# Layer 1's bias sums placed amid the first block's products, and its second factor transposed into other PSUM pools

## The chip, the cores and the metric

The kernel runs on one core of one Trainium2 chip. The metric is the device time of one execution in microseconds (us); the figure used is the median of several executions. The core's engines are named as the profile names them: PE (TensorE, with PEld for its weight loads), DVE (VectorE), ACT (ScalarE), POOL (GpSimd) and SP (SyncE, which here only issues transfers). Each engine works through its own queue of instructions; semaphores order them against one another.

## The reference

A stack of four graph layers over 128 graphs of 64 nodes with 512 features, all in float32. Every layer starts with a layer norm and a ReLU and adds its result to x. The two layers that the change touches:

```python
# layer 0: h = relu(layernorm(x))
qk = h @ Wqk;  q, k = split(qk);  v = h @ Wv
agg = einsum('bij,bjd->bid', adj, k * mask)
w = mask * einsum('bid,bid->bi', q, agg) / sqrt(512)
x = x + softmax(w, axis=1)[:, :, None] * v

# layer 1: h = relu(layernorm(x))
query = h @ Wq.T + bq;  key = h @ Wk.T + bk;  value = h @ Wv.T + bv
weight = adj * exp(query @ key.T)
x = x + (weight / weight.sum(axis=2, keepdims=True)) @ value
```

Layer 2 is an attention with eight heads, layer 3 a three-step graph propagation. Neither is touched.

## The kernel before, in words

The 8192 tokens are cut into 32 blocks of 256 tokens (two tiles of 128). Blocks go through layers 0 and 1 in pairs, in the order of the list `steps`: layer 0 of blocks 0 and 1, layer 1 of blocks 0 and 1, layer 0 of blocks 2 and 3, and so on. Layers 2 and 3 follow. A block's products with 512x512 weights are made by seven half-size products with sums (a scheme of Strassen's kind): `sums` (L204) forms the sums of the activations on POOL, `formed` (L86) those of the weights, and `Product` (L223) issues the matmuls, with its two PSUM tiles called ab and dc. Of a product, `first` and `second` are the early matmuls, after which `keep_ab` (L276) saves a part through ACT (p, L280) and DVE (u, L281); `late` (L296) adds the rest and `store` (L300) writes the result through ACT (L302), DVE (L303 to L305) and POOL (L306). The late matmuls of a tile can't start before `keep_ab` has read it. `side_by_side` (L346) issues two such products together; its list `between` holds actions for three places amid them: after the first product's early part, ahead of the first late part, ahead of the second.

A query and its key meet only in a product, so both projections of a layer are folded into one weight. That is setup work. For layer 0 it stands in `setup0` (L438), for layer 1 in `setup1` (L446). `setup1` is a generator. Its first part loads the two 512x512 factors qT and kT, the two bias rows (b1qk) and the value weight. The factors go into the weight slots 4 and 5, which layer 0's factors used, so their loads wait until layer 0's fold has been made. Its second part

- makes nine sums on DVE (L467), each a product of 128x512 elements with an accumulated sum: four columns of qT with the key's bias (u1), four of kT with the query's bias (c1), and the product of the two biases (d1);
- sends c1 through DRAM and back as a row on all partitions (L473, L475);
- transposes both factors on PE (`transpose_weight`, L411: 16 transposes into four PSUM tiles, tw_q and then tw_k, which four copies put back into the factor in place, two on DVE, L422, and two on ACT, L420);
- multiplies them (`folded`, L424: four PSUM tiles pf of 512 columns, each from four matmuls, copied out half by ACT, L434, and half by DVE, L435);
- forms the weight sums on POOL and asks for layer 2's weights.

The nine sums share a buffer tag ("agg") with the neighbour sums of layer 0. PSUM is cut into three pools: `ps_tr` with two tiles (tag "tr": transposed activations, layer 0's neighbour sums pa), `ps_mm` with four (tag "mm": ab and dc of the products, tw and pf of the setup), and `ps_sc` with two (tag "sc": scores, sums over a graph).

In the main loop the second part of `setup1` is asked for after layer 0 of block 0 and ahead of layer 0 of block 1:

```python
for i, (layer, b) in enumerate(steps):
    if i == 1:
        made1 = next(setup)
```

Layer 0's own end of a block (`layer0_end`, L526: a sum over the graph on PE, sm_w, L400, then the softmax on ACT and DVE and the addition to x) is kept in the list `open_end` and issued amid the next block's products, so for block 0 amid block 1's. Within what the program text allows, a scheduler places the instructions in each engine's queue. In the queues before, PE has for this stretch: the late products of block 0, tw_q, pa of block 1, sm_w of block 0, tw_k, pf, and the products of block 1. DVE has: the last sums of block 0's products, L511, the nine sums with wd (L518) behind the first of them, the copies of q, the start of the softmax, the copies of k. ACT has: two copies of q, the copies of pa, the softmax with two copies of k amid it.

Of the kernel before, what the change touches and what calls it, by code (L numbers as in the profile page):

```python
# [8 lines left out]
FP = mybir.dt.float32  # L9
AF = mybir.ActivationFunctionType  # L10
ALU = mybir.AluOpType
AX = mybir.AxisListType

P = 128
N = 64
D = 512
K = D // P
# [8 lines left out]
def kernel(ctx: ExitStack, tc: tile.TileContext, a: dict, out: bass.AP):  # L26
# [7 lines left out]
    nc = tc.nc  # L34
# [7 lines left out]
    med = ctx.enter_context(tc.tile_pool(name="med", bufs=3))  # L42
    snap = ctx.enter_context(tc.tile_pool(name="snap", bufs=2))
    small = ctx.enter_context(tc.tile_pool(name="small", bufs=3))
    ps_tr = ctx.enter_context(tc.tile_pool(name="ps_tr", bufs=2, space=bass.MemoryType.PSUM))
    ps_mm = ctx.enter_context(tc.tile_pool(name="ps_mm", bufs=4, space=bass.MemoryType.PSUM))
    ps_sc = ctx.enter_context(tc.tile_pool(name="ps_sc", bufs=2, space=bass.MemoryType.PSUM))
# [32 lines left out]
    def slot(place: int, name: str):  # L80
        return wpool.tile([P, 7, 2, F], FP, tag=f"w{place}", name=name)
# [3 lines left out]
    def formed(w, engine):  # L85
        for to, x, y in sums_of_weights:  # L86
            engine.tensor_tensor(w[:, to], w[:, x], w[:, y], ALU.subtract)
# [3 lines left out]
    def later(w):  # L91

        chores.extend((w, s) for s in sums_of_weights)
# [7 lines left out]
    def fetched(name: str, place: int, queue):  # L101
        w = slot(place, name)
        for i in range(2):
            for j in range(2):
                queue.dma_start(
                    w[:, quarters[i][j]],
                    a[name][i * F : (i + 1) * F, j * F : (j + 1) * F].rearrange(
                        "(k p) o -> p k o", p=P
                    ),
                )  # L110
        return w
# [16 lines left out]
    def factor(ap, which: str, layer: int, queue):  # L128

        w = slot({"q": 4, "k": 5}[which], f"{which}_{layer}")  # L130
        w = w.rearrange("p s k o -> p (s k o)")[:, : K * D].rearrange("p (k o) -> p k o", k=K)
        for k in range(K):
            queue.dma_start(w[:, k, :], ap[k * P : (k + 1) * P, :])
        return w
# [4 lines left out]
    f0 = [  # L139
        factor(a["L0_Wqk"][:, i * D : (i + 1) * D], c, 0, queue)  # L140
        for i, (c, queue) in enumerate((("q", nc.scalar), ("k", nc.sync)))
    ]
# [254 lines left out]
    def graph_sums(e, cols: int, name: str):  # L397

        ps = ps_sc.tile([P, cols], FP, tag="sc", name=f"sm_{name}")
        nc.tensor.matmul(ps, ones_bd, e, start=True, stop=True)  # L400
        return ps
# [6 lines left out]
        return r  # L408


    def transpose_weight(w, name: str):  # L411

        pts = [ps_mm.tile([P, K, P], FP, tag="mm", name=f"tw_{name}_{m}") for m in range(K)]
        for k in range(K):
            for m, pt in enumerate(pts):
                nc.tensor.transpose(pt[:, k, :], w[:, k, m * P : (m + 1) * P], ident)
        for m, pt in enumerate(pts):
            flat = pt.rearrange("p k i -> p (k i)")
            if m % 2:
                nc.scalar.copy(w[:, m, :], flat)  # L420
            else:
                nc.vector.tensor_copy(w[:, m, :], flat)  # L422

    def folded(aT, bT, layer: int, place: int):  # L424

        m = slot(place, f"fold{layer}")
        for i in range(K):
            pm = ps_mm.tile([P, D], FP, tag="mm", name=f"pf_{layer}_{i}")
            for k in range(K):
                nc.tensor.matmul(  # L430
                    pm, aT[:, k, i * P : (i + 1) * P], bT[:, k, :],
                    start=(k == 0), stop=(k == K - 1),
                )
            nc.scalar.copy(m[:, quarters[i // 2][0], i % 2, :], pm[:, :F])  # L434
            nc.vector.tensor_copy(m[:, quarters[i // 2][1], i % 2, :], pm[:, F:])  # L435
        return m

    def setup0():  # L438
# [7 lines left out]
    def setup1():  # L446


        qT, kT = (factor(a[f"L1_W{c}"], c, 1, nc.sync) for c in "qk")

        bias = big.tile([P, 2, P, K], FP, tag="v", name="b1qk")
        for i, n in enumerate(("L1_bq", "L1_bk")):
            nc.sync.dma_start(
                bias[:, i], a[n].rearrange("(o p) k -> o p k", o=1).to_broadcast([P, P, K])
            )
        w1v = fetched("L1_Wv", 3, nc.sync)
        yield
        u = const.tile([P, K], FP, tag="u1", name="u1")
        cc = small.tile([P, K], FP, tag="cc", name="c1", bufs=1)
        d = const.tile([P, 1], FP, tag="d1", name="d1")  # L460
        for to, x, by in (
            *((u[:, k : k + 1], qT[:, k, :], 1) for k in range(K)),
            *((cc[:, k : k + 1], kT[:, k, :], 0) for k in range(K)),
            (d, None, 1),
        ):
            junk = med.tile([P, P, K], FP, tag="agg", name="bias1", bufs=2)
            nc.vector.scalar_tensor_tensor(  # L467
                junk, bias[:, 0] if x is None else x.rearrange("q (k p) -> q p k", k=K), 1.0,
                bias[:, by], ALU.mult, ALU.mult, accum_out=to,
            )  # L470

        crow = tc.dram_tile([1, D], FP, name="c1_row")
        nc.sync.dma_start(crow.rearrange("o (k p) -> p (o k)", p=P), cc)  # L473
        c1 = const.tile([P, 2, D + 1], FP, tag="u3", name="c1")[:, 0, :D]
        nc.sync.dma_start(c1, crow.to_broadcast([P, D]))  # L475
        for w, c in zip((qT, kT), "qk"):
            transpose_weight(w, f"{c}1")
        m = folded(kT, qT, 1, 2)
        formed(m, nc.gpsimd)
        formed(w1v, nc.gpsimd)  # L480
        w2 = [fetched(f"L2_W{c}", 4 + i, nc.sync) for i, c in enumerate("qk")]
        for w in w2:
            later(w)
        yield m, u, c1, d, w1v, w2
# [41 lines left out]
    def layer0_end(b: int, x, gv, w, wd):  # L526
        wrow = graph_sums(wd.rearrange("p t i -> p (t i)"), TT * N, f"w_{b}")
        mn = small.tile([P, TT], FP, tag="mx0", name=f"mn0_{b}")
        nc.vector.tensor_reduce(
            mn, wrow.rearrange("p (t i) -> p t i", t=TT), AX.X, ALU.min  # L530
        )
        nc.vector.tensor_tensor(w, w, mn, ALU.subtract)
        tot = small.tile([P, TT], FP, tag="tot", name=f"tot_{b}")
        for t in range(TT):
            nc.scalar.activation(
                wd[:, t, :], wrow[:, t * N : (t + 1) * N], AF.Exp, bias=mn[:, t : t + 1],
                scale=-1.0, accum_out=tot[:, t : t + 1],
            )
        ex = small.tile([P, TT], FP, tag="ex", name=f"ex_{b}")
        nc.scalar.activation(ex, w, AF.Exp, scale=-1.0)  # L540
        att = small.tile([P, TT], FP, tag="att", name=f"att_{b}")
        nc.vector.reciprocal(att, tot)
        nc.vector.tensor_tensor(att, att, ex, ALU.mult)
        for t in range(TT):
            nc.vector.scalar_tensor_tensor(
                x[:, t, :], gv[:, 1, t, :], att[:, t : t + 1], x[:, t, :], ALU.mult, ALU.add
            )
# [364 lines left out]

    prepare(0)
    transpose_weight(f0[0], "q0")
    turned(0)
    transpose_weight(f0[1], "k0")
    m0, msc = setup0()
    formed(w0v, nc.gpsimd)
    loaded[1] = load_x(1, x_d[rows(1), :], 0), load_adjT(1, 0)
    setup = setup1()  # L920
    next(setup)
    open_end = []
    for i, (layer, b) in enumerate(steps):
        if i == 1:
            made1 = next(setup)
        between = [[], [chore], []]
        for n, end in open_end:
            between[n].append(end)
        if i + 1 < len(steps):
            between[0].append(lambda: prepare(i + 1))  # L930
            between[2].append(lambda: turned(i + 1))
        else:
            between[0].append(lambda: prepare2(0))
            between[2].append(lambda: turned2(0))
        if layer == 0:
            softmax = layer0(b, *loaded[b], *normed[i], between)
            open_end = [(0, lambda b=b, softmax=softmax: layer0_end(b, *softmax))]
        else:
            attention = layer1(b, *loaded[b], *normed[i], between)
            open_end = [  # L940
                (1, lambda b=b, a=attention: layer1_end(b, loaded[b][0], *a, x1[b]))
            ]
        if i == len(steps) - 3:
            made2 = setup2()
# [7 lines left out]
    def layer3_step(b: int, ahead: bool = True):  # L952
# [20 lines left out]
    qk, ops = layer2_in(0, normed2[0], [  # L973
        [lambda: prepare2(1), chore], [*(end for _, end in open_end), chore], [lambda: turned2(1)]
    ])
# [8 lines left out]
    for b in range(n_blk):  # L984
        x = loaded2[b][0]
# [7 lines left out]
        if b + 1 < n_blk:  # L993
            qk, ops = layer2_in(b + 1, normed2[b + 1], [[], [lambda: chore(1 if b else 2)]])
# [99 lines left out]
```

## Time and profile before

| what | us |
|---|---|
| median of three executions | 2693.18 (2690.39 to 2693.68) |
| the profiled execution | 2690.4 |
| its span, from the first to the last instruction | 2688.6 |
| PE busy in the span | 2646.6 |
| layer 1's setup on PE, from tw_q to the first product of block 1 | 43.77 to 73.78 |

A line of the timeline gives the start, the duration, the engine, the line of the program and the operation, what is written and what is read, the shape and the count, and in brackets the idle time of that engine just before with what ended it. A line of the windows view gives a stretch, its length, the busy time of PE, PEld, DVE, ACT and POOL with the number of instructions, then PE's granted clock as a share of full speed, the share of time that the transfer engines were busy, and their rate in GB/s. A line of the waits view gives who waited, for whom, the time in all, how often, and the longest. A float32 matmul shows as two matmul records for each instruction of the program, a transpose as one. The end of a matmul record is modelled, so records that follow one another overlap a little.

### The profile page before, as it was taken

The page shows a single profiled execution, that of the slowest core. Times are in us where ns is not written, and L with a number is a line of the kernel's source. Part 1 is how long each engine was busy: PE and PEld are TensorE (multiplying, and loading weights), DVE is VectorE, ACT ScalarE, POOL GpSimd, SP SyncE. Part 2 cuts the span into 40 slices and gives each one's busy share as a digit, 9 for nine tenths or more (in the row PEclk, how much of TensorE's full clock was granted, in tenths as well). Part 3 has the DMA queues.
Part 4 walks back from the last instruction along what each step waited for, and adds up shares of the span by engine and source line. Part 5 has one row for each costly group of instructions (what it writes and reads, how often), then busy time and mean ns, then how long its engine had stood idle before and what let it go on. Part 6 is the DMA issues. An engine that isn't in the chain of part 4 may idle for free.

```text
span 2688.6 us, 52721 instructions
## 1 busy us (share of the span) xinstructions
PE 2646.6 (98%) x20752; PEld 2256.7 (84%) x20752; DVE 1682.3 (63%) x4398; ACT 942.7 (35%) x2290; POOL 1274.9 (47%) x1585
## 2 busy tenths in 40 slices
PE   8999999999999999999999999999999999999999
PEld 5888888888888888898999999999877777777776
DVE  5566666666666666555655655555666666666664
ACT  2333334333433333333333333333323333333332
POOL 3443333333334344655654565555564544444454
PEclk9999999999999999999999999999999999999999
DMA  4200111111101112111111111111211111111110
GB/s 155 69 35 34 34 34 35 42 43 37 47 34 34 34 66 78 37 52 37 39 45 44 39 37 52 37 39 52 72 50 46 56 51 51 51 51 51 51 50 32
DMA packets 103165, 129.81 MB, mean 48 GB/s; under 512 B 40834, under 2 KB 50050, under 8 KB 102916
## 3 DMA queue, kind: packets, MB, share of 16 engines
q1 hardware_dynamic: 102340, 125.38, 14.0%
q8 instruction: 163, 2.67, 0.4%
q10 hardware_dynamic: 576, 1.05, 0.1%
q14 instruction: 86, 0.70, 0.1%
HBM read 76.07 MB, written 50.34 MB: 47 GB/s over the span
## 4 chain that ended last, share of the span: by engine, by line
PE 77%; DVE 11%; DMA 5%; POOL 3%; ACT 2%; issue 2%; POOLq 0%; SPq 0%; ACTq 0%; DVEq 0%
PE ab_v L251 10%; PE ab_y L251 10%; PE dc_v L251 8%; PE dc_y L251 7%; PE ab_g L244 4%; PE ab_g L251 4%; DMA x<-x 4%; PE dc_g L244 3%; PE ab_q L244 3%; PE dc_g L251 3%; PE ab_k L244 3%; PE po L392 3%; PE tr L190 3%; PE dc_k L244 2%; PE dc_q L244 2%; DVE e L662 2%
## 5 line engine op out<-in xcount | busy, mean ns | idle before, releaser
L179 ACT ACTIVATE h<-x,nmr,rstd 128x512 f32<-128x512 f32 x256 | 194.4, 806 | 212.7 <-DVE nmr L174 208.8
L167 DVE BATCH_NORM_STATS2 stats<-x 128x6 f32<-128x512 f32 x256 | 167.3, 675 | 75.4 <-DMA x<-x 71.1
L172 POOL TENSOR_TENSOR rstd<-ve,neghalf 128x2 f32<-128x2 f32 x128 | 89.5, 699 | 260.8 <-DVE ve L170 260.5
L251 PE MATMUL ab_y<-L_Wk,hT 128*128 128x256 f32 x768 | 206.2, 391 | 3.6 <-DVE u_y L303 2.6
L251 PE MATMUL ab_v<-L_Wv,hT 128*128 128x256 f32 x768 | 202.8, 387 | 4.8 <-DVE stats L167 3.7
L251 PEld LDWEIGHTS ab_y<-L_Wk,hT 128*128 128x128 f32 x768 | 136.1, 190 | 75.9 <-issue 25.1
L251 PE MATMUL ab_v<-L_Wv,S 128*128 128x256 f32 x768 | 198.0, 381 | 0.0
L251 PE MATMUL ab_y<-L_Wk,S 128*128 128x256 f32 x768 | 197.9, 380 | 0.0
L251 PE MATMUL dc_v<-L_Wv,S 128*128 128x256 f32 x768 | 197.3, 380 | 0.0
L251 PE MATMUL dc_y<-L_Wk,S 128*128 128x256 f32 x768 | 193.8, 381 | 0.2 <-DVE u_y L851 0.2
L251 PEld LDWEIGHTS dc_y<-L_Wk,S 128*128 128x128 f32 x768 | 146.2, 191 | 21.4 <-DVE u_y L851 1.7
L251 PEld LDWEIGHTS ab_v<-L_Wv,S 128*128 128x128 f32 x768 | 146.8, 191 | 19.9
L872 POOL TENSOR_TENSOR tz<-tz,y 128x512 f32<-128x512 f32 x63 | 91.3, 1449 | 146.1 <-ACT tz L869 146.1
L251 PEld LDWEIGHTS dc_v<-L_Wv,S 128*128 128x128 f32 x768 | 143.8, 191 | 18.8 <-issue 0.8
L251 PEld LDWEIGHTS ab_y<-L_Wk,S 128*128 128x128 f32 x768 | 144.1, 191 | 18.1
L251 PEld LDWEIGHTS ab_v<-L_Wv,hT 128*128 128x128 f32 x768 | 136.5, 191 | 22.9 <-ACT qk L323 7.5
L190 PE MATMUL tr<-ident,h 128*128 128x128 f32 x1024 | 134.3, 275 | 0.4 <-ACT h L179 0.4
L190 PEld LDWEIGHTS tr<-ident,h 128*128 128x128 f32 x1024 | 119.4, 142 | 11.2 <-ACT h L179 0.8
L216 POOL TENSOR_TENSOR S<-hT 128x256 f32<-128x256 f32 x128 | 100.8, 788 | 38.4 <-ACT hT L193 36.0
L326 POOL TENSOR_TENSOR qk<-u_q,p_q 128x256 f32<-128x256 f32 x32 | 23.3, 727 | 195.5 <-DVE u_q L310 195.5
L281 DVE TENSOR_TENSOR u_v<-ab_v,p_v 128x256 f32<-128x256 f32 x96 | 40.6, 423 | 109.7 <-ACT p_v L280 109.7
L219 POOL TENSOR_TENSOR S<-hT 128x256 f32<-128x256 f32 x128 | 107.0, 836 | 1.2
(238 smaller groups left out, 6472.6 us busy)
## 6 DMA issues: line engine op xcount, KB each, us to landing
x<-x SPq DMA_DIRECT2D x128, 512.0 KB, 3.4
x<-in_x_dram SPq DMA_DIRECT2D x32, 512.0 KB, 3.5
out_dram<-x SPq DMA_DIRECT2D x31, 512.0 KB, 2.8
adjT<-in_adjT_dram SPq DMA_DIRECT2D x64, 64.0 KB, 1.9
adjq<-in_adj_dram SPq DMA_DIRECT2D x64, 64.0 KB, 2.3
L_Wk<-in_L_Wk_dram SPq DMA_DIRECT2D x16, 256.0 KB, 5.2
L_Wv<-in_L_Wv_dram SPq DMA_DIRECT2D x12, 256.0 KB, 5.1
q<-in_L_Wqk_dram ACTq DMA_DIRECT2D x4, 256.0 KB, 5.4
```

The costliest lines, as they stand in the source:

```text
L167: nc.vector.bn_stats(stats[:, t, :], x[:, t, :])
L172: nc.gpsimd.tensor_tensor(rstd, ve, neghalf, ALU.pow)
L179: nc.scalar.activation(h, x[:, t, :], AF.Relu, bias=nmr[:, t : t + 1], scale=rstd[:, t : t + 1])
L190: nc.tensor.transpose(pt[:, k, :], h[:, k * P : (k + 1) * P], ident)
L216: nc.gpsimd.tensor_tensor(S1, A21, A22, ALU.add)
L219: behind[0] = nc.gpsimd.tensor_tensor(S3, A11, A21, ALU.subtract)
L244: nc.tensor.matmul(dst[:, m * P : (m + 1) * P], w[:, place, k, m * P : (m + 1) * P], left[:, k, :], start=key not in self.begun, stop=last ...
L251: nc.tensor.matmul(dst, left[:, k, :], w[:, place, k, :], start=key not in self.begun, stop=last and k == 1, skip_group_check=True,)
L281: self.kept = nc.vector.tensor_tensor(self.u2, self.b, self.p1, ALU.add)
L392: nc.tensor.matmul(ps[t][half[g ^ t]], e[half[g], t, :], us[t][half[g]], start=True, stop=True)
L662: nc.vector.tensor_tensor(eh, eh, mx.unsqueeze(2).to_broadcast([P, TT * hq, N]), ALU.subtract)
L872: nc.gpsimd.tensor_tensor(tz[t], tz[t], y0[:, t, :], ALU.add)
```

## The change

Four things change in the text.

1. `setup1` is cut into more parts. Its nine sums are asked for within layer 0 of block 0: d1 and the four sums of qT ahead of the first late products, the four of kT and the transfers of c1 ahead of the second late products. They use buffers of the tag "e2" (three) in place of "agg" (two).
2. `transpose_weight` takes the PSUM pool and tag of each of its four tiles, and which of its copies go to ACT. Layer 1's first factor keeps the "mm" tiles and has all four copies on ACT; its second factor goes into two "tr" and two "sc" tiles, with two copies on each of DVE and ACT as before.
3. `folded` takes an action that is issued behind its first PSUM tile. For layer 1 this is `layer0_end` of block 0, which is taken out of `open_end`.
4. Layer 0's second factor goes into two "sc" and two "mm" tiles.

```diff
-    def transpose_weight(w, name: str):
+    def transpose_weight(w, name: str, places=((ps_mm, "mm"),) * K, on_scalar=(1, 3)):
 
-        pts = [ps_mm.tile([P, K, P], FP, tag="mm", name=f"tw_{name}_{m}") for m in range(K)]
+        pts = [
+            pool.tile([P, K, P], FP, tag=tag, name=f"tw_{name}_{m}")
+            for m, (pool, tag) in enumerate(places)
+        ]
...
-            if m % 2:
+            if m in on_scalar:
...
-    def folded(aT, bT, layer: int, place: int):
+    elsewhere = ((ps_tr, "tr"), (ps_sc, "sc")) * 2
+
+    def folded(aT, bT, layer: int, place: int, amid=lambda: None):
...
+            if not i:
+                amid()
...
-        for to, x, by in (
-            *((u[:, k : k + 1], qT[:, k, :], 1) for k in range(K)),
-            *((cc[:, k : k + 1], kT[:, k, :], 0) for k in range(K)),
-            (d, None, 1),
-        ):
-            junk = med.tile([P, P, K], FP, tag="agg", name="bias1", bufs=2)
...
+        def dots(*sums):
+            for to, x, by in sums:
+                junk = med.tile([P, P, K], FP, tag="e2", name="bias1", bufs=3)
+                nc.vector.scalar_tensor_tensor(
+                    junk, x, 1.0, bias[:, by], ALU.mult, ALU.mult, accum_out=to
+                )
...
+        dots((d, bias[:, 0], 1))
+        dots(*((u[:, k : k + 1], x, 1) for k, x in enumerate(columns(qT))))
+        yield
+        dots(*((cc[:, k : k + 1], x, 0) for k, x in enumerate(columns(kT))))
...
-        for w, c in zip((qT, kT), "qk"):
-            transpose_weight(w, f"{c}1")
-        m = folded(kT, qT, 1, 2)
+        yield
+        transpose_weight(qT, "q1", on_scalar=range(K))
+        transpose_weight(kT, "k1", elsewhere)
+        m = folded(kT, qT, 1, 2, lambda: layer0_end(0, *softmax))
...
-    transpose_weight(f0[1], "k0")
+    transpose_weight(f0[1], "k0", ((ps_sc, "sc"),) * 2 + ((ps_mm, "mm"),) * 2)
...
+        between = [[], [chore], []]
+        if i == 0:
+            for n in (1, 2):
+                between[n].append(lambda: next(setup))
         if i == 1:
+            open_end.clear()
             made1 = next(setup)
-        between = [[], [chore], []]
```

In the queues that result, PE has for this stretch: the late products of block 0, tw_q, tw_k, sm_w of block 0, pf, pa of block 1, the products of block 1. DVE has d's sum between the statistics of block 1, seven of the other eight sums on either side of the first u_v (L281) and ahead of u_g (L281) of block 0, and the last behind u_g. ACT has four copies of q, two of k, the softmax, and the copies of pa behind those of pf. POOL and SP keep their order.

## The prediction

> **What bounds the kernel now.** I read the page's busy line first, then the busy time of three stretches, then who TensorE (PE) waited for in the first 74 us, then the timeline of the gap, and last its clock.
>
> ```profile
> PE 2646.6 (98%) x20752; PEld 2256.7 (84%) x20752; DVE 1682.3 (63%) x4398; ACT 942.7 (35%) x2290; POOL 1274.9 (47%) x1585
> ```
> ```profile
> 0.00:43.77 43.77, 37.90 (x145) 25.10 (x145) 16.82 (x37) 12.76 (x24) 18.91 (x29) 1.00 0.75 237
> 43.77:73.78 30.01, 22.73 (x75) 11.69 (x74) 18.25 (x45) 7.42 (x17) 3.75 (x5) 0.83 0.06 10
> 73.78:300.00 226.22, 226.22 (x1629) 192.83 (x1628) 150.16 (x402) 86.97 (x223) 96.79 (x123) 1.00 0.14 45
> ```
> PE is the bound nearly everywhere: from 73.78 us on it doesn't pause for 226 us. The stretch 43.77 to 73.78 us is layer 1's setup: PE stands still for 30.01 - 22.73 = 7.28 us and has only 0.83 of its clock. What is won here moves all later work forward. Whom PE waited for in the first 74 us:
>
> ```profile
> PE tw_q L416 <- DMA q<-in_L_Wqk_dram: 5.3, 3, 4.6
> PE tw_k L416 <- DVE q L422: 3.3, 1, 3.3
> PE tw_k L416 <- ACT q L420: 2.4, 2, 1.2
> PE sm_w L400 <- DVE wd L518: 1.5, 1, 1.5
> ```
> The first is the first load; the other three, 7.2 us, are the gap. PE's timeline there (start, duration, group, in brackets the idle time before and what ended it):
>
> ```profile
> 43.77 2.07 PE L416 MATMUL tw_q<-ident,q 128*128 128x128 f32 x16
> 45.76 1.09 PE L392 MATMUL pa<-h,am 64*64 64x512 f32 x8
> 48.31 0.49 PE L400 MATMUL sm_w<-wd,ones_bd 128*128 128x128 f32 x2 [1.46 <-DVE wd L518]
> 50.01 0.66 PE L416 MATMUL tw_k<-ident,k 128*128 128x128 f32 x4 [1.21 <-ACT q L420]
> 51.86 1.12 PE L416 MATMUL tw_k<-ident,k 128*128 128x128 f32 x4 [1.19 <-ACT q L420]
> 56.25 1.97 PE L416 MATMUL tw_k<-ident,k 128*128 128x128 f32 x8 [3.27 <-DVE q L422]
> 58.36 15.59 PE L430 MATMUL pf<-q,k 128*128 128x512 f32 x32
> 73.78 1.03 PE L251 MATMUL dc_g<-fold,S 128*128 128x256 f32 x4
> ```
> The tw_k transposes need the four "mm" PSUM tiles that tw_q filled; the copies that empty these stand behind the nine bias sums on VectorE (DVE):
>
> ```profile
> 47.02 1.02 DVE L467 SCALAR_TENSOR_TENSOR bias<-q,b1qk 128x512 f32<-128x512 f32 x1
> ...
> 54.88 0.69 DVE L467 SCALAR_TENSOR_TENSOR bias<-b1qk 128x512 f32<-128x512 f32 x1
> 55.50 0.09 DVE L467 DVE_READ_ACCUMULATOR bias<-b1qk 128x1 f32 x1
> 55.50 1.29 DVE L422 COPY q<-tw_q 128x512 f32<-128x512 f32 x2
> ```
> And the clock, in a second call by stretch (here PE's busy time, then the clock):
>
> ```profile
> 48.31:51.30 2.99, 1.14 (x6) 1.00 0.01 3
> 51.30:58.36 7.06, 3.09 (x13) 0.50 0.04 0
> 58.36:61.70 3.34, 3.34 (x4) 0.52 0.00 0
> ```
>
> **What the Trainium skill says.** "TensorE: Matmul & The Clock Gate", section "What's actually happening": after about one idle window of 3.4 us PE falls to half clock and needs about as long of sustained work to get it back. The trace agrees: idle from 46.85 us with little work between, 0.50 from 51.3 us, full again about 61.7 us, 3.3 us after pf starts. "PSUM — Partial Sum Buffer", section "Engine vs sequencer instructions": ScalarE, VectorE and GpSimd queues are strict first in, first out, and matmuls run in program order. The trace agrees (the q copies wait until 55.50 us), so a sum that waits for its load holds all of DVE behind it. "Perfetto Trace Analysis", section "Tensor Engine Instruction (MATMUL, LD_WEIGHTS)": the end of a matmul is modelled. So I use differences of starts.
>
> **The gap's budget.** PE's work in it at full clock, start to start: 16 tw_q transposes 1.99 (43.77 to 45.76); 16 tw_k the same, 1.99; pa 1.02 (117.10 to 118.12, a later block); sm_w 0.22 (88.53 to 88.75); 32 pf matmuls 13.93 (15.76 to 29.69, layer 0's fold). Sum 19.15 of 30.01 us, so 10.86 us are lost, 1.49 of them (15.42 - 13.93) as slow clock inside pf. More than 10.86 can't be won here.
>
> **The change part by part.** Behind its first 140 or so instructions the order on every engine is the same as before; only what follows differs.
>
> (1) *The nine sums move into block 0's products.* DVE's queue becomes: d's sum between block 1's two statistics aggregations; sums q0, q1 behind layer 0's weight sums (end 32.76); then u_v (L281), sums q2, q3, k0, k1, k2, then u_g (L281), sum k3, then u_v (L303). Eight sums cost 0.96 each (start to start, 49.13 to 50.09), d's 0.62. Cover: between 32.76 and 43.51 us DVE is mostly idle in the trace. But each sum waits for its chunk of the factor. These loads are issued at 29.83 to 33.1 us, once layer 0's fold has read the slots; landing 2.7, 3.0, 3.9, 4.9 (q) and 5.2, 5.5, 5.6, 5.8 us (k) later, about 32.5, 33.2, 34.6, 36.1, 36.9, 37.6, 38.2, 38.9. Stepping through: q0 32.76, q1 33.72, u_v 34.68 to 35.1, q2 35.0, q3 36.1 (waits), k0 37.06, k1 38.02, k2 38.98, u_g 39.94 to 40.4, k3 40.3, u_v (L303) 41.25, gv 41.8 and 42.1, hT copy 42.45 to 43.1. Who waits: block 0's late ab_v products (37.71 us) for u_v, 2.6 us of slack; its late ab_g products (41.17) for u_g, 0.8 us of slack; both hold. u_g's second sum (L303) waits for ScalarE (ACT) until 43.51 anyway, so DVE has caught up and the tw_q tiles come free as before: cost 0 on PE. d's sum waits for the bias rows (issued 12.44 and 13.20, landing 4.6 and 5.1 later, 18.3); it ends about 18.95, ahead of block 1's rstd on POOL (20.94): 0. The row of c1 leaves earlier on the SP queue (about 42 instead of 55.0): 0.
> POOL runs the v half's L306, then block 1's four sums S, then L306 of the g half: the later hT copy pushes this last from 44.90 to about 45.35, and layer 0's L511 on DVE from 45.66 to about 46.1; two of 0.70 each, then wd about 47.6 to 47.9 (before 47.97 to 48.25).
>
> (2) *tw_k goes to the "tr" and "sc" PSUM pools.* Their last readers (hT copies, 43.1) are done, the k loads too. So tw_k follows tw_q at 45.76, full clock, and ends at 47.75. The waits of 1.21, 1.19 and 3.27 us go.
>
> (3) *All four q copies on ACT.* ACT's queue: q0 to q3, k1, k3. From about 45.6 at 0.49 to 0.53 start to start (57.83, two in 1.07) the four end near 47.7; k1 follows once tw_k has ended, 47.8 to 48.4; k3 to 48.9. DVE copies k0 and k2 behind wd, 47.9 to 49.2.
>
> (4) *The softmax's sm_w now follows tw_k.* It needs wd (47.9) and an "sc" tile, so ACT's k1 copy (48.4): this is late next. PE idles from 47.75 to about 48.45, 0.7 us. Bounds: not under 0.6 (one copy of 0.58 behind the last transpose), up to 1.3 if ACT starts at 46.1 and pays 0.58 for each of five copies. I take 0.7. It is far from an idle window, so the clock stays.
>
> (5) *pf, then pa.* pf starts at 48.7 (k0 and q are there; its third and fourth steps, from 50.4 on, find k2 and k3), ends at 62.63; pa 1.02 after it, dc_g at 63.65. In the trace dc_g starts at 73.78. Gain 10.1 us. Layer 0's end runs beside pf: 49.3 plus its 10.4 us (mn 56.70 to h 67.1) is 60, and its transposes come only at 73. POOL's sums of the folded weights follow pf by the same distance as before.
>
> (6) *Layer 0's second factor partly in "sc" tiles.* tw_k at 12.06 follows the transposes without a wait in the trace: 0, bounds 0 to -0.3 us.
>
> **Sum.** 10.86 - 0.7 = 10.1 us. The profiled execution took 2690.4 us (span 2688.6); it would take 2680.3 (span 2678.5). Their median is 2693.18, 2.8 above it: 2693.18 - 10.1 = 2683.1 us. Copies and waits bound the gain between 9.5 and 10.9, the three times before spread over 3.3 us.
>
> **Rivals.**
> (B) *The sums hold PE at block 0's late products.* If the chunks land L later than in the trace, ab_g is late by L - 0.8. For: DMA is 0.68 busy in 30 to 40 us and the margin is small. Against: queue and load order are unchanged, and all such loads land within 6.6 us of issue. With L = 5 the gain is 10.1 - 4.2 = 5.9: 2687.3 us.
> (C) *Slower.* The same place, further out: u_g behind seven sums on DVE, PE idle in front of ab_g past the clock's window, about 1.7 us more for a cold restart (3.4 us at half speed). It eats the gain from L = 0.8 + 10.1 - 1.7 = 9.2, that is k2 landing at 47 us. At L = 15: 14.2 + 1.7 - 10.1 = 5.8 lost, 2699.0 us. For: every sum waits in order. Against: no load in the trace is that late.
> (D) *The time doesn't reach the end*: later waits take it back. For: PE waits 20.9 us after 74 us. Against: each of these waits moves along with the work (the loads behind the 3.7 us for stats are issued by that work too), and until 300 us there is none. Then about 2692 us.
>
> **How the numbers follow.** A change under 0.2% (5.4 us) can't be told from none. Forecast 0.83, B 0.08, D 0.05, C 0.04. Range: 2683.1, by the bounds and the spread, 2680 to 2686.5; down to 2679 and up to 2688 takes in most of B. Faster: the forecast and most of B, 0.89; same: D and the rest of B, 0.07; slower 0.04.
>
> **What would show it.** Right: tw_k directly behind tw_q, one wait of about 0.7 us before sm_w, clock 1.00 throughout 43 to 65 us, dc_g of block 1 near 63.7 us. Wrong: idle time before ab_g near 41 us with a DVE sum or u_g as its releaser (B, C); a clock of 0.50 anywhere after 40 us; dc_g early but the span unchanged (D).

## The result, and the profile after

| | before | changed |
|---|---|---|
| median, six executions each, same chip | 2690.98 | 2682.44 |
| median, another chip (17 and 5 executions) | 2693.85 | 2682.11 |
| profiled execution | 2690.4 | 2682.39 |
| its span | 2688.6 | 2680.6 |
| from tw_q to block 1's dc_g on PE | 30.01 | 19.75 |

The changed kernel is faster: the ratio is 0.9965, with a 95% interval of 0.9954 to 0.9975 on the first chip, and 0.9960 (0.9947 to 0.9974) on the second. The forecast, 2693.18 - 10.1, is a ratio of 0.9962 and lies in both.

The windows view of the changed kernel, cut at the same two events as before (columns: the stretch, its length, busy time of PE, PEld, DVE, ACT and POOL with counts, granted clock, DMA share, GB/s):

```profile
0.00:41.60 41.60, 35.71 (x144) 23.13 (x145) 25.90 (x55) 12.58 (x24) 18.89 (x28) 1.00 0.80 249
41.60:61.35 19.75, 19.15 (x75) 9.89 (x73) 9.24 (x26) 6.72 (x17) 4.24 (x6) 1.00 0.04 14
```

In the second stretch PE is busy for 19.15 of 19.75 us at full clock. DVE's nine sums have gone to the first stretch: its busy time there is 25.90 us, where before it was 16.82, and 9.24 in place of 18.25 in the second. Whom PE waits for in the first 66 us (waits view):

```profile
PE tw_q L419 <- DMA q<-in_L_Wqk_dram: 5.6, 2, 5.2
PE sm_w L400 <- ACT k L423: 0.6, 1, 0.6
```

Of 7.2 us of waiting in the gap, 0.6 are left, for the copy that the forecast named. PE's timeline:

```profile
41.60 2.07 PE L419 MATMUL tw_q<-ident,q 128*128 128x128 f32 x16
43.51 1.91 PE L419 MATMUL tw_k<-ident,k 128*128 128x128 f32 x16
46.02 0.49 PE L400 MATMUL sm_w<-wd,ones_bd 128*128 128x128 f32 x2 [0.60 <-ACT k L423]
46.41 14.00 PE L435 MATMUL pf<-q,k 128*128 128x512 f32 x32
60.34 1.09 PE L392 MATMUL pa<-h,am 64*64 64x512 f32 x8
```

tw_k stands behind tw_q without a bracket, and pf takes 14.00 us in place of 15.59, so the clock is kept as well. On DVE, the place that two rivals pointed at:

```profile
36.79 1.05 DVE L472 SCALAR_TENSOR_TENSOR bias<-k,b1qk 128x512 f32<-128x512 f32 x1
37.76 0.09 DVE L472 DVE_READ_ACCUMULATOR bias<-k,b1qk 128x1 f32 x1
37.76 0.43 DVE L281 TENSOR_TENSOR u_g<-ab_g,p_g 128x256 f32<-128x256 f32 x1
```

u_g ends at 38.19 us; block 0's late ab_g products start at 39.01. The margin is 0.82 us.

The two profiles don't differ by the setup alone. The changed one starts tw_q 2.17 us earlier, gains 10.26 us in the setup, and has 12.4 us of lead at block 1, but its span is only 8.0 us shorter: the last 3252 matmul records, nearly all of them layer 3, take 609.6 us in place of 605.6. The repeats below deal with that.

### The profile page after: what moved, and what is told of

It is laid out like the page before. It is cut to its first block, busy times and chain, and to the rows that moved or that the text cites. A ratio compares the mean times of both kernels' runs of the same rounds, so it can differ in the third digit from the quotient of the medians.

```text
span 2680.6 us, 52719 instructions
## 1 busy us (share of the span) xinstructions
PE 2642.7 (99%) x20752; PEld 2250.3 (84%) x20752; DVE 1683.3 (63%) x4396; ACT 944.2 (35%) x2292; POOL 1276.9 (48%) x1585
## 4 chain that ended last, share of the span: by engine, by line
PE 72%; DVE 12%; DMA 7%; POOL 4%; ACT 3%; issue 2%; SPq 0%; ACTq 0%; DVEq 0%; POOLq 0%
PE ab_v L251 10%; PE dc_v L251 8%; PE ab_y L251 8%; PE dc_y L251 5%; DMA x<-x 5%; PE ab_g L244 4%; PE ab_g L251 4%; PE dc_g L244 3%; PE dc_g L251 3%; PE ab_k L244 3%; PE ab_q L244 3%; PE po L392 3%; PE tr L190 3%; PE dc_k L244 2%; PE dc_q L244 2%; DVE e L675 2%
## 5 line engine op out<-in xcount | busy, mean ns | idle before, releaser
L281 DVE TENSOR_TENSOR u_v<-ab_v,p_v 128x256 f32<-128x256 f32 x96 | 40.6, 423 | 108.0 <-ACT p_v L280 108.0
```

The source lines that it names most:

```text
L281: self.kept = nc.vector.tensor_tensor(self.u2, self.b, self.p1, ALU.add)
```

## The experiments

Each kernel's stretch from tw_q to dc_g is read off PE's timeline as above. The ratios are against the kernel before, run beside it.

**The buffers of the sums alone.**

```diff
-            junk = med.tile([P, P, K], FP, tag="agg", name="bias1", bufs=2)
+            junk = med.tile([P, P, K], FP, tag="e2", name="bias1", bufs=3)
```

> The kernel before with one line changed: the nine sums write their products into buffers of tag e2 (three) instead of agg (two). Nothing is asked for earlier in the text and the PSUM pools stay, but the queues then hold the sums amid block 0's products. Theory Q (the sums in DVE's queue ahead of the copies were the whole obstacle): tw_k waits only for the q copies, about 1.5 us in all; from tw_q to block 1's dc_g about 20.5 us in place of 30.0 (19.75 in the changed kernel), clock 1.00; time 8 to 10 us under before. Theory P (the other PSUM pools make the gain): tw_k still has to wait until its four tiles are emptied, the stretch stays above 26 us and the time falls by less than 4 us.

Measured: ratio 0.9982 (0.9976 to 0.9989), 4.8 us less (4.5 between the medians); the stretch is 23.03 us, 7.0 less. PE's timeline of that kernel:

```profile
44.45 2.12 PE L416 MATMUL tw_q<-ident,q 128*128 128x128 f32 x16
46.50 1.07 PE L392 MATMUL pa<-h,am 64*64 64x512 f32 x2
47.50 0.44 PE L416 MATMUL tw_k<-ident,k 128*128 128x128 f32 x2
49.45 3.25 PE L416 MATMUL tw_k<-ident,k 128*128 128x128 f32 x14 [1.51 <-DVE q L422]
52.63 1.08 PE L392 MATMUL pa<-h,am 64*64 64x512 f32 x6
53.64 14.00 PE L430 MATMUL pf<-q,k 128*128 128x512 f32 x32
```

One line of the program, with no word on when the sums are asked for, moves all nine sums amid block 0's products. In the old buffers, by the program, they could not go there: the tag "agg" has two, which layer 0's neighbour sums hold until L511 has read them. (Whether "e2" needs its third buffer, no run shows.) Theory Q had the waits right (1.51 us) and the sum wrong. The wait cost PE its clock, so the 14 transposes behind it take 3.18 us, start to start, where 14/16 of 1.99, that is 1.74, were due; the two parts of pa, split apart, take 1.00 and 1.01 instead of 1.02 together; and the softmax, still amid block 1, now holds u_g there, for which PE waits 1.7 us behind the stretch (waits view: ab_g from DVE's u_g), so that part of the 7.0 us is lost again. Theory P's number for the time (under 4 us) is missed as well, and its 26 us for the stretch too: both parts matter.

**The pools without the sums.** All of the change, but the sums asked for behind block 0 and in the old buffers:

```diff
-                junk = med.tile([P, P, K], FP, tag="e2", name="bias1", bufs=3)
+                junk = med.tile([P, P, K], FP, tag="agg", name="bias1", bufs=2)
...
-        if i == 0:
-            for n in (1, 2):
-                between[n].append(lambda: next(setup))
         if i == 1:
             open_end.clear()
+            next(setup), next(setup)
             made1 = next(setup)
```

> The changed kernel with the nine sums back behind block 0's products (asked for there, and in buffers of tag agg), all else as changed: tw_k in the tr and sc pools, four q copies on ACT, the softmax amid the fold, pa behind it. Theory Q: tw_k follows tw_q at once, but the copies of q and k wait behind the sums (to about 55.5 us on DVE in the profile before), so PE idles about 8 us ahead of sm_w and pf, long enough to lose its clock to 0.50; block 1's dc_g about 1 us earlier than in the kernel before counted from tw_q (29 against 30.0), the time 0 to 2 us under before. Theory P: the stretch falls to 22 us or less and the time by 6 us or more.

Measured: ratio 0.9996 (0.9988 to 1.0005), not to be told from none; the stretch is 28.91 us.

```profile
46.95 1.91 PE L419 MATMUL tw_k<-ident,k 128*128 128x128 f32 x16
55.75 0.80 PE L400 MATMUL sm_w<-wd,ones_bd 128*128 128x128 f32 x2 [6.89 <-ACT k L423]
57.53 15.49 PE L435 MATMUL pf<-q,k 128*128 128x512 f32 x32 [0.97 <-DVE k L425]
```

tw_k is at once behind tw_q, and then PE waits for the same sums one step later, 6.89 us in one piece, and loses its clock (pf 15.49). Theory Q holds here to 0.1 us. The two parts don't add: in the stretch they are worth 7.0 and 1.1 us alone and 10.3 together, in the times 4.8, nothing that shows, and some 10, because each leaves a wait in place that the other removes.

**The margin in front of ab_g.** The four sums of q made twice:

```diff
-        dots(*((u[:, k : k + 1], x, 1) for k, x in enumerate(columns(qT))))
+        for _ in range(2):
+            dots(*((u[:, k : k + 1], x, 1) for k, x in enumerate(columns(qT))))
```

> The changed kernel with the four sums of q made twice (the results are the same), so 13 sums in DVE's queue, 8 of them ahead of u_g of block 0 and 11 ahead of the second u_v. Theory of the margin (the sums are free only as long as u_g ends ahead of block 0's late ab_g products; in the changed kernel 37.76 + 0.43 = 38.2 against 39.0 us): one more sum of 0.97 us ahead of u_g uses the 0.8 us up, and the four late sums of k then hold the tiles of tw_q: PE waits 2.5 to 4 us in all between block 0's late products and tw_q, with DVE as the releaser, and dc_g of block 1 is that much later. Rival (DVE has slack to spare there): no new wait of PE over 0.3 us.

Measured, one execution. PE's timeline:

```profile
38.62 1.04 PE L190 MATMUL tr<-ident,h 128*128 128x128 f32 x8
39.64 1.13 PE L251 MATMUL ab_g<-fold,hT 128*128 128x256 f32 x4
...
42.90 0.33 PE L419 MATMUL tw_q<-ident,q 128*128 128x128 f32 x1 [0.40 <-DVE u_v L303]
44.52 0.33 PE L419 MATMUL tw_q<-ident,q 128*128 128x128 f32 x1 [1.29 <-DVE gv L305]
45.45 3.25 PE L419 MATMUL tw_q<-ident,q 128*128 128x128 f32 x14 [0.60 <-DVE u_g L303]
```

ab_g starts 1.02 us after the transposes where 0.87 is usual (38.14 to 39.01 in the changed kernel): one sum of 0.97 us uses up the 0.82 us and 0.15 us show, as the margin says. The late sums then hold tw_q's tiles for 0.40 + 1.29 + 0.60 us. In all 2.4 us, just under the 2.5 us expected at least, and behind them the transposes run at half clock (14 in 3.04 us). From block 0's late dc_g to block 1's dc_g it is 24.68 us in place of 20.61. The sums' cover is real and nearly used up.

**The buffers and pools alone, nothing asked for elsewhere.** To the kernel before, three changes: the tag e2, tw_k in "tr" and "sc" tiles, and the four q copies on ACT (first kernel) or two on each engine as before (second).

```diff
-            junk = med.tile([P, P, K], FP, tag="agg", name="bias1", bufs=2)
+            junk = med.tile([P, P, K], FP, tag="e2", name="bias1", bufs=3)
...
-        for w, c in zip((qT, kT), "qk"):
-            transpose_weight(w, f"{c}1")
+        transpose_weight(qT, "q1", on_scalar=range(K))
+        transpose_weight(kT, "k1", ((ps_tr, "tr"), (ps_sc, "sc")) * 2)
```

> The kernel before with three things changed and nothing asked for elsewhere: the sums' buffers of tag e2, tw_k in the tr and sc pools, the four q copies on ACT. The sums are still asked for behind block 0 and the softmax still amid block 1; the queues nevertheless come out as in the changed kernel, but for d's sum, which stands ahead of the second u_v. Theory Q2 (the buffers and pools are what makes the gain, the places in the text aren't): 19.7 to 20.3 us from tw_q to dc_g, time within 2 us of the changed kernel's (ratio near 0.996). Rival (the places matter): the stretch longer than 21 us or the gain under 7 us.

Measured: 0.9964 (0.9951 to 0.9978), the stretch 20.26 us, as Q2 has it. PE waits 0.96 us for wd in front of sm_w, since d's sum stands later, ahead of the second u_v. That is all that the new places in the text add: 0.5 us of a stretch, nothing that the times can show.

> The same with the q copies split as before, two on DVE and two on ACT. On DVE the two come behind layer 0's L511 sums, which end about 1.7 us after tw_q, and push the copies of k by 1.3 us: pf starts 1 to 1.4 us later than in the changed kernel, 20.7 to 21.3 us from tw_q to dc_g, clock still 1.00; 1 us less gain than with all four on ACT. If ACT's four copies were the last wait, the split would be as fast or faster (19.2 to 19.7 us).

Measured: 0.9974 (0.9964 to 0.9984), the stretch 23.02 us: in the direction expected, by more than twice the size (1 us less gain was expected; it is 2.8 in the stretch and 2.6 between the medians). The waits are nearly as reckoned, 1.42 us in front of sm_w and 0.65 in front of pf, which starts 1.6 us later than in the changed kernel. But they took the clock, which was expected to hold (windows view, PE's busy time and the clock):

```profile
45.77:47.19 1.42, 0.00 (x1) 1.00 0.00 0
47.19:48.30 1.11, 0.46 (x2) 1.00 0.00 0
48.30:49.00 0.70, 0.70 (x1) 0.51 0.00 0
```

pf takes 15.68 us there. So the copies on ACT are worth 2.8 us of the stretch, 1.7 of them as clock.

**Layer 0's second factor in other tiles**, alone and taken out of the change; and both kernels once more:

```diff
-    transpose_weight(f0[1], "k0")
+    transpose_weight(f0[1], "k0", ((ps_sc, "sc"),) * 2 + ((ps_mm, "mm"),) * 2)
```

> The kernel before with one thing changed: layer 0's second factor goes into two sc and two mm tiles; the queues are the same as before. Theory Z: 29.6 to 30.0 us from tw_q to dc_g, the time of the kernel before within 2 us. Theory B: the setup as before, layer 3 some 3 us longer (609 to 610 us in place of 605 to 607), the time 2 to 4 us above before.

> The changed kernel with layer 0's second factor transposed into four mm tiles again, all else as changed. The queues are the same as in the changed kernel; only which PSUM banks the later mm tiles get differs, by two places, and is again as in the kernel before. Theory Z (that part is worth nothing): 19.7 us from tw_q to dc_g, the same time as the changed kernel within 2 us, and no wait ahead of layer 0's tw_k. Theory B (the shifted banks are what made layer 3 some 3 us longer in both profiles of the changed kernel): layer 3's last 605 to 607 us as in the kernel before, and 2 to 3 us less than the changed kernel in all.

> The kernel before, profiled a second time. Theory V (what the two profiles differ by outside the setup is variation from execution to execution): the start of tw_q of layer 1, 43.77 us in the first profile, moves by up to 2 us, and the length of layer 3 (from about 2160 us to the end) moves by up to 4 us. Theory R (they belong to the change): tw_q starts at 43.8 within 0.3 us and layer 3 has the length it had within 0.5 us.

> The changed kernel, profiled a second time. Within the setup both theories expect 19.75 us from tw_q to dc_g within 0.3 us. Theory V: the start of tw_q, 41.60 us in the first profile, moves by up to 2 us, and layer 3, 4 us longer than in the kernel before in the first pair of profiles, has another length. Theory R: tw_q at 41.6 within 0.3 us and layer 3 again about 4 us longer than in the kernel before.

> The changed kernel once more, beside the others on one chip, so that it can be compared with them. The forecast's sum says 10.1 us under before (ratio 0.9962); the setup 19.7 us from tw_q to dc_g. Theory B: layer 3's last part 609 to 610 us; theory V (variation from execution to execution): anywhere from 605 to 610 us.

Measured, the profiles of these kernels together (us; the time from which PE first has its full clock by the trace's record, layer 0's first pf, tw_q of layer 1, the stretch from there to dc_g, and the last 3252 matmul records):

| kernel | full clock from | layer 0's pf at | tw_q at | stretch | last records |
|---|---|---|---|---|---|
| before | 13.80 | 15.76 | 43.77 | 30.01 | 605.6 |
| before, again | 12.39 | 15.12 | 43.13 | 29.64 | 607.4 |
| other tiles alone | 11.29 | 14.34 | 42.35 | 29.46 | 609.9 |
| changed | 8.74 | 13.59 | 41.60 | 19.75 | 609.6 |
| changed, again | 16.66 | 17.25 | 45.26 | 19.69 | 609.2 |
| changed, third | 12.63 | 15.27 | 43.28 | 19.67 | 607.5 |
| changed without them | 12.63 | 15.28 | 43.29 | 19.66 | 606.9 |

The stretch repeats within 0.1 us in the changed kernel. The first 43 us don't: layer 0's fold starts anywhere from 13.6 to 17.3 us, and earliest and latest are the same kernel. What differs is when PE first gets its full clock: in all twelve profiles, the later that is, the later the fold starts.

Layer 3 varies by 4 us, and here Theory B (shifted PSUM banks lengthen layer 3) is right about the length. The last records take 607.5 to 609.9 us in all six profiles with the other tiles (609.6 with the pools alone, 607.9 with four more sums) and 605.6 to 607.4 in all six without them (606.1 with the buffers alone, 606.0 and 605.9 in the two small kernels). But the 2 to 4 us more that Theory B expects of the time don't come: other tiles alone 0.9997 (0.9989 to 1.0005), changed without them 0.9961 (0.9949 to 0.9974) beside 0.9960 for the changed kernel. What layer 3 loses, about 2.6 us on average, comes back ahead of it: from block 1's dc_g to the last records it takes 2.2 us less on average with the other tiles (1999.4 to 2004.6 us against 2002.1 to 2007.7). So that part is worth nothing in the time. How the tiles do this, through the banks or otherwise, is not settled.

## Why the prediction was right

The mechanism and its size both held, so step by step:

- *The budget.* PE's work in the gap was put at 19.15 us. PE's busy time in the stretch is now 19.15 us. That the hundredths agree is luck: the transposes take 0.16 us less from start to start than reckoned, sm_w 0.17 more.
- *(1) The sums.* 0.96 us each was forecast, 0.97 to 0.98 measured; d's sum, forecast at 0.62, took 1.12, and nothing on PE waited for it. A slack of 0.8 us in front of ab_g, 0.82 measured; no cost on PE, none measured. The loads landed sooner after their issue than in the profile before (q after 2.5 to 3.5 us in place of 2.7 to 4.9, k after 3.9 to 4.8 in place of 5.2 to 5.9), so no sum had to wait for its chunk, as the forecast had for q3. That the cover is no larger than this the kernel with four more sums showed.
- *(2) tw_k.* Directly behind tw_q, 1.91 us after its start, against 1.99.
- *(3) The copies on ACT.* Forecast: the four q copies in about 2.1 us, then k1 as soon as tw_k ends. ACT's copies of q take 2.06 us and k1 starts right behind them, as tw_k ends:

```profile
43.42 2.06 ACT L423 COPY q<-tw_q 128x512 f32<-128x512 f32 x4 [2.11 <-PE tw_q L419]
45.34 1.12 ACT L423 COPY k<-tw_k 128x512 f32<-128x512 f32 x2
```

What the step did not say is why this matters: in the small kernel with two of the copies on DVE, PE waits 2.1 us in all, and half speed follows.

- *(4) The new last wait.* Forecast 0.7 us in front of sm_w for ACT's k1 copy; measured 0.60, for that copy.
- *(5) pf and pa.* Forecast: dc_g 19.88 us after tw_q (63.65 - 43.77); measured 19.75. Gain in the setup 10.1 forecast, 10.26 between the two first profiles, 9.95 between the second ones (29.64 - 19.69).
- *(6) Layer 0's tiles.* Forecast 0 to -0.3 us; the pair of experiments shows no effect on the time. The step looked at layer 0 alone; that the tiles move layer 3 and what is ahead of it by over 2 us each, in opposite directions, it did not see.
- *The time.* Forecast 10.1 us less; 8.5 between the medians of the first chip, 11.7 on the second, with the variation of the first 43 us and of layer 3 (up to 4 us each) on top of the setup's nearly fixed 10 us. That the forecast time itself, 2683.1, lies 0.7 us from the median is partly luck: the kernel before has 2690.98 over six executions, not the 2693.18 of the first three. The upper bound of the gain, 10.9, left out the step's own least wait of 0.6 us; by the forecast's own terms it is 10.3, or 10.6 with step (6). And a change under 0.2% could be told from none: the buffers alone, 0.18%.

The rivals: B and C fell, since u_g stayed ahead of ab_g; D fell with the time: 8.5 and 11.7 us less, where D has about 1. In the first pair of profiles the lead is 12.4 us at block 1, 12.2 at about 1000 us, 12.0 ahead of layer 3 and 7.9 at the end; in the third profile of the changed kernel, against the same one before, it falls only from 10.8 to 9.2. The experiments add what the forecast left together: the move of the sums comes from their buffers, not from the places where the text asks for them, and the sums and the pools are worth their 10 us only together.

The place where the argument was lucky is the clock. It took the 0.7 us of idle time to be safe because it is short beside a window of 3.4 us, the figure of the Trainium skill ("TensorE: Matmul & The Clock Gate", section "What's actually happening"). The 0.60 us that came were safe, but 1.3 us were not in the kernel with the buffers alone; the measurement decides. What the clock follows in these traces stands in the last section.

## What to carry to other kernels

Where a scheduler orders the queues, look at what a step's buffers are shared with before moving the step in the text: here two buffers of a shared tag held nine sums back, and another tag alone brought them forward. When a wait is removed, follow the waiting engine to its next wait before counting the gain; two changes that each give a fraction alone may give all of it together. And price an idle time of PE with its clock: waits of 1.5 to 2.3 us cost another 1.3 to 1.7 us at half speed.

## What was not expected of the hardware

PE's clock fell after idle times well under the 3.4 us of the page, and not at one fixed length. In the kernel with the buffers alone it fell within 1.3 us of idle time (idle from 47.94 us, half clock from 49.23). With the pools alone it held through nearly 5 us (idle from 48.86 us, full clock until 53.73), and 0.60 and 0.96 us (the changed kernel, the first of the two small ones) didn't touch it.

The page ("TensorE: Matmul & The Clock Gate", section "What's actually happening") calls its window free-running, so where the idle time falls in it could explain the spread. The traces bear this out. In each of the twelve profiles all changes of the clock lie whole multiples of 3.413 us apart, though that grid lies elsewhere in each execution. Here are stretches cut at the grid, with PE's busy time and the clock: two each of the buffers alone and of the pools alone, then one each of the second of the small kernels and of the changed one:

```profile
45.81:49.23 3.42, 2.13 (x11) 1.00 0.00 0
49.23:52.64 3.41, 3.19 (x16) 0.50 0.00 0
46.90:50.31 3.41, 1.96 (x18) 1.00 0.01 2
50.31:53.73 3.42, 0.00 (x0) 1.00 0.00 0
44.90:48.31 3.41, 1.34 (x11) 1.00 0.00 0
42.88:46.29 3.41, 2.81 (x25) 1.00 0.00 0
```

The pools' first stretch is busy for 1.96 us and keeps the clock; the next is idle, and at its end the clock falls. The small kernel's is busy for 1.34 us, and the clock falls; the changed kernel's for 2.81, and it holds. Over all profiles the clock falls 33 times ahead of the program's end, 32 of them behind a stretch that was busy for 0.43 of its length or less; it held over one stretch of 0.43 and over every one of 0.48 and more but one. That one is the first above, 2.13 us or 0.62: 1.0 us of it is pa, whose matmuls use 64x64 blocks, and that such work counts for less is a guess. This is read off the traces; no run moved an idle time against the grid.

The clock's column does not show the state at the start: between 10 and 12 us eight transposes take 1.97 us in eight of the twelve profiles, at a stated clock of 1.00, where the same eight take 1.04 us later. The trace's own record of the clock begins only when it becomes full, 8.7 to 16.7 us after the start, and the column counts the time ahead of that as 1.00.
